# Two products of a graph layer by Strassen's scheme: seven products of quarters for eight, in stage 0 of a float32 kernel

## The chip, the cores and the metric

The kernel runs on one core of one Trainium2 chip. The metric is the device time of one execution in microseconds (us); less is better. The core has five queues that run side by side, each in its own order: PE (matrix products; PEld is its weight load), DVE (vector operations), ACT (activations), POOL (general operations, and one of the issuers of transfers) and SP (issues transfers). Matrix products land in PSUM[...]; everything else works in SBUF.

## The reference

Two graph attention layers over 4096 nodes with 512 features. Each normalizes its rows, takes the positive part, applies its attention and adds the result to its input. Only the first layer is touched, and of it the part before the attention:

```python
h = jnp.maximum(_layernorm(x, axis=-1), 0.0)       # rows, 4096 x 512
node_att = jax.nn.softmax(h @ node_w, axis=0)      # one weight a node
he = h @ edge_w                                    # 512 x 512 weights
e = jnp.where(adj > 0, he @ he.T, NEG_BIG)
edge_att = jax.nn.softmax(e, axis=1)
support = h @ weight                               # 512 x 512 weights
output = adj * (node_att * edge_att) @ support + bias
x = x + output
```

(The names h and he are changed here so that they agree with the kernel's.) The change concerns the two products `h @ edge_w` and `h @ weight`.

## The kernel before

The program has stages, one after the other: stage 0 (rows, the two products, node logits), stage B (scores of all pairs of blocks, from L289), stage C (softmax and attention of the first layer, from L364), and then the second layer. Each stage opens its own buffers in memory that the stage before has released.

Stage 0 is written with a fixed order: each queue executes what the Python code emits, in that order. The 4096 rows are 32 tiles of 128 rows (index t); four tiles make a block of 512 rows (index b, eight blocks). A tile goes through these functions:

- `fetch` (L130): SP loads the tile `xt` from `x`. There are 8 buffers.
- `stats` (L134): DVE computes mean and variance (L136, L138), ACT the deviation `sd` (L140).
- `norm` (L142): DVE computes `rs` and `mr` (L144, L146); ACT normalizes and takes the positive part in one activation, giving `h` (L149, L151).
- `logit` (L153): DVE multiplies `h` with the node weights and sums (`acc_z`, L154); POOL adds the bias to `xt` into a buffer `xb` (L157) and stores it (L158).
- Turning the tile so that features lie on the partitions. For the first two blocks (t < `T0` = 8) PE transposes and DVE copies (L188, L189). For the others `send` (L168) stores `h` in squares of 32, `pull` (L174) loads them back as `hq`, and DVE transposes inside the squares (L181). Both write into the block's tile `h_t`.

A finished block is then multiplied twice. `support(t)` (L192) makes one tile of `h @ weight`: four float32 matmuls of 512 columns into one bank, which DVE copies into `sup` (L198). `edges(b, d)` (L200) makes 128 features of `h @ edge_w`, turned, in the same way; ACT copies the bank into `he_t` (L205). Each product of a block has 16 matmuls of 512 columns. Banks come in three names (`pt`, `ps`, `pe`) with two buffers each.

`step(t)` (L216) places the tile work: around each `edges(b, j)` of block b it fetches, normalizes four tiles ahead, sends, turns one tile of block b+1, pulls two tiles ahead and takes statistics five tiles ahead. A block therefore is: four `edges` with four steps between, then the four `support` of the next block.

```python
for b in range(NB):
    for j in range(TB):
        edges(b, j)
        step((b + 1) * TB + j)
    if b + 1 < NB:
        for j in range(TB):
            support((b + 1) * TB + j)
```

Behind the loop come a few small operations on the node logits (L257 to L269), whose end releases the memory that the first loads of stage B use.

Of the functions that a comparison needs: L331 are the score matmuls of stage B; its tiles on the diagonal have 512, 384, 256 and 128 columns. L336, L343 and L344 are DVE's operations on these scores. L451 (DVE) and L461 (POOL) both use the result of the activation L445 in stage C.

Of the kernel before, what the change touches and what calls it, by code (L numbers as in the profile page):

```python
# [28 lines left out]
def kernel(  # L29
# [71 lines left out]
    with tc.tile_pool(name="w0", bufs=1) as wp, tc.tile_pool(name="a0", bufs=2) as ap_, tc.tile_pool(  # L101
        name="a0s", bufs=8
    ) as sp, tc.tile_pool(name="a0p", bufs=2, space=PSUM) as pp, tc.manual_schedule():
        we = wp.tile([P, KC, F], FP, name="we")
# [8 lines left out]

        pw = pp.tile([P, KC, P], FP, name="pt")
        for k in range(KC):
# [4 lines left out]
        T0 = 2 * TB  # L120
        nw_s = mb_0

        def squares_of(h):
# [6 lines left out]
        def fetch(t):  # L130
            xts[t] = sp.tile([P, F], FP, name="xt", bufs=8)
            nc.sync.dma_start(xts[t], x[t * P:(t + 1) * P, :])
# [9 lines left out]
        def norm(t):  # L142
            rs = sp.tile([P, 1], FP, name="rs")
            nc.vector.reciprocal(rs, sds.pop(t))  # L144
            mr = sp.tile([P, 1], FP, name="mr")
            nc.vector.scalar_tensor_tensor(mr, mvs.pop(t)[:, 0:1], -1.0, rs, op0=ALU.mult, op1=ALU.mult)  # L146
            hs[t] = sp.tile([P, F], FP, name="h", bufs=5)
            if t < T0:
                nc.scalar.activation(hs[t], xts[t], AF.Relu, bias=mr, scale=rs)  # L149
            else:  # L150
                nc.scalar.activation(squares_of(hs[t]), columns_of(xts[t]), AF.Relu, bias=mr, scale=rs)  # L151

        def logit(t, h):  # L153
            nc.vector.tensor_tensor_reduce(acc_z, h, nw_b if t < T0 else nw_s, 1.0, 0.0, ALU.mult, ALU.add,  # L154
                                           lg[:, t:t + 1])
            xb = sp.tile([P, F], FP, name="xb", bufs=1)
            nc.gpsimd.tensor_tensor(xb, xts.pop(t), bias_b, ALU.add)  # L157
            nc.gpsimd.dma_start(xb_d[t * P:(t + 1) * P, :], xb)  # L158
# [17 lines left out]
        def turn(t):  # L176
            b, j = divmod(t, TB)
            if j == 0:
                hts[b] = ap_.tile([P, KC, BL], FP, name="h_t")
            if t >= T0:  # L180
                nc.vector.transpose(  # L181
                    hts[b][:, :, j * P:(j + 1) * P].rearrange("p k (a q) -> p k a q", q=S),
                    hqs.pop(t).rearrange("p (a k q) -> p k a q", k=KC, q=S))
                return
            h = hs.pop(t)
            pt = pp.tile([P, KC, P], FP, name="pt")
# [13 lines left out]
        def edges(b, d):  # L200
            pe = pp.tile([P, BL], FP, name="pe")
            for k in range(KC):
                nc.tensor.matmul(pe, we[:, k, d * P:(d + 1) * P], hts[b][:, k, :],  # L203
                                 start=(k == 0), stop=(k == KC - 1))
            nc.scalar.copy(he_t[b][:, d, :], pe)  # L205


# [20 lines left out]
        upto(stats, 2)  # L228
        upto(norm, 1)
        turn(0)  # L230
        upto(stats, 3)
        upto(norm, 2)
        turn(1)
        support(0)
        upto(norm, 3)
        turn(2)
        support(1)
        upto(stats, 5)
        upto(norm, 4)
        turn(3)  # L240
        support(2)
# [17 lines left out]
        m2 = sp.tile([P, 1], FP, name="m2")  # L259
        nc.gpsimd.partition_all_reduce(m2, m1, P, bass_isa.ReduceOp.max)  # L260
        m3 = sp.tile([P, 1], FP, name="m3")
        nc.vector.tensor_scalar(m3, m2, -1.0, None, ALU.mult)
        s1 = sp.tile([P, 1], FP, name="s1")
        nc.scalar.activation(na, lg, AF.Exp, bias=m3, accum_out=s1)
        s2 = sp.tile([P, 1], FP, name="s2")
        nc.gpsimd.partition_all_reduce(s2, s1, P, bass_isa.ReduceOp.add)
        s3 = sp.tile([P, 1], FP, name="s3")
        nc.vector.reciprocal(s3, s2)
# [838 lines left out]
```

## Time and profile before

| what | value |
|---|---|
| device time, three runs | 2943.97, 2947.51 and 2948.33 us; median 2947.51 |
| the profiled execution | 2943.79 us; its span, first to last instruction, 2941.9 us |
| busy in the span | PE 2885.6, DVE 2536.9, ACT 1317.9, POOL 1410.4 us |
| stage 0, stretch 0 to 240.7 us | PE 227.84, PEld 103.15, DVE 102.13, ACT 52.37, POOL 61.53 us busy |
| L196 (`support`), L203 (`edges`) | 256 records each, 596 and 592 ns mean |

In the profile a line such as `L203 PE MATMUL pe<-h_t,we 128*128 128x512 f32 x256` is a group of instructions of one line of the kernel: its engine, what it writes and reads, its shape and count. A float32 matmul has two records. Records of PE overlap, since matmuls are pipelined, so the distance between starts tells more than the length of one. In a list in order of time the first number is the start in us from the span's start, the second the length; in brackets stands how long the engine was idle before and what it waited for. In a table of stretches each engine has its busy us and the number of its instructions; behind them stand the granted clock of PE (1.00 is full), the share of the transfer engines, and GB/s.

### The profile page before, as it was taken

What the parts mean: (1) busy time and instruction counts of PE and PEld (TensorE: products, weight loads), DVE (VectorE), ACT (ScalarE), POOL (GpSimd) and SP (SyncE); (2) the same over time, 40 slices, a digit from 0 to 9 for tenths busy, and PEclk for the clock granted to TensorE, in tenths of its full rate; (3) what the DMA queues carried; (4) which work ended last, traced back from release to release, by engine and by line L of the source; (5) the groups of instructions that cost most, each with busy time, mean ns of one, the idle gap of its engine ahead of it and who ended that gap; (6) DMA issues with size and microseconds to landing.
All of it is one profiled execution on the core that took longest, in us unless ns stands there. A gap on an engine that the chain in (4) does not pass through costs nothing.

```text
span 2941.9 us, 42890 instructions
## 1 busy us (share of the span) xinstructions
PE 2885.6 (98%) x14987; PEld 1144.6 (39%) x14987; DVE 2536.9 (86%) x3606; ACT 1317.9 (45%) x1817; POOL 1410.4 (48%) x1075
## 2 busy tenths in 40 slices
PE   8999999999999999999999989999999999999998
PEld 4444444444444444444444423333322223232223
DVE  5435777778898998998996789999999999999998
ACT  2211111111122222222221068888777777777776
POOL 3401111113444434444444756676766676767675
PEclk9999999999999999999999999999999999999999
DMA  5525666667877766756754269899989898999796
GB/s 182 172 79 201 223 218 224 226 218 182 208 169 194 189 158 199 193 159 189 203 168 136 58 181 237 239 225 239 232 236 233 238 233 236 234 237 235 209 227 168
DMA packets 517032, 587.66 MB, mean 200 GB/s; under 512 B 291832, under 2 KB 344088, under 8 KB 516816
## 3 DMA queue, kind: packets, MB, share of 16 engines
q1 hardware_dynamic: 460336, 410.90, 46.8%
q0 software_dynamic: 54464, 170.10, 26.1%
q10 hardware_dynamic: 2016, 3.93, 0.4%
q8 instruction: 117, 1.92, 0.3%
q14 instruction: 99, 0.81, 0.1%
HBM read 418.91 MB, written 73.60 MB: 167 GB/s over the span
## 4 chain that ended last, share of the span: by engine, by line
PE 73%; DVE 11%; ACT 7%; issue 4%; DMA 3%; POOL 1%; SPq 0%; DVEq 0%; ACTq 0%; POOLq 0%
PE po L481 28%; PE pe L331 15%; PE pv L886 14%; DVE pr L855 9%; PE dn L891 4%; PE po L592 4%; ACT e L823 3%; PE pe L203 3%; PE ps L196 3%; DMA acc<-pr 2%; ACT rl L841 1%; ACT ex L813 1%; DVE pr L852 1%; DMA xb_d<-xb 1%; DMA eb<-e_d 0%
## 5 line engine op out<-in xcount | busy, mean ns | idle before, releaser
L886 PE MATMUL pv<-pr,sup 128*32 128x512 f32 x8192 | 1023.6, 594 | 14.0 <-POOL d_m L1051 5.6
L481 PE MATMUL po<-sup,at 128*128 128x512 f32 x2048 | 884.1, 594 | 7.2 <-DMA eb<-e_d 6.1
L864 POOL TENSOR_TENSOR acc<-acc,pr 128x1024 f32<-128x1024 f32 x240 | 583.6, 2431 | 328.0 <-DVE pr L855 326.1
L855 DVE SCALAR_TENSOR_TENSOR pr<-z,g_m,ex 128x1024 f32<-128x1024 f32 x512 | 630.9, 1273 | 5.6 <-ACT ex L813 5.6
L481 PEld LDWEIGHTS po<-sup,at 128*128 128x128 f32 x2048 | 389.4, 191 | 493.8 <-issue 452.4
L461 POOL TENSOR_TENSOR racc<-racc,ex 128x512 f32<-128x512 f32 x240 | 354.2, 1476 | 388.2 <-ACT ex L445 386.8
L886 PEld LDWEIGHTS pv<-pr,sup 128*32 128x32 f32 x8192 | 300.8, 110 | 606.3 <-issue 509.3
L445 ACT ACTIVATE ex<-d 128x512 f32<-128x512 f32 x256 | 160.5, 630 | 611.5 <-DVE d L443 606.3
L331 PE MATMUL pe<-he_t,he_t 128*128 128x512 f32 x896 | 386.4, 592 | 0.0
L813 ACT ACTIVATE ex<-e 128x1024 f32<-128x1024 f32 x256 | 263.4, 1029 | 241.7 <-DVE pr L855 241.6
L891 PE MATMUL dn<-pr,d_m 128*2 128x512 f32 x1984 | 348.7, 592 | 0.0
L855 DVE SCALAR_TENSOR_TENSOR pr<-z,g_m,e 128x1024 f32<-128x1024 f32 x256 | 327.8, 1280 | 0.2 <-ACT e L823 0.2
L852 DVE SCALAR_TENSOR_TENSOR pr<-rl,ngd_m,ex 128x1024 f32<-128x1024 f32 x224 | 285.3, 1274 | 12.0 <-ACT ex L813 11.7
L823 ACT ACTIVATE e<-e,ld_m 128x1024 f32<-128x1024 f32 x256 | 291.3, 1138 | 0.0
L841 ACT ACTIVATE rl<-z,ngd_m,d_m 128x1024 f32<-128x1024 f32 x224 | 275.6, 1230 | 0.0
L335 POOL DMA_DIRECT2D e_d<-es x144 | 78.6, 546 | 364.6 <-ACT es L334 359.1
L331 PEld LDWEIGHTS pe<-he_t,he_t 128*128 128x128 f32 x896 | 169.6, 190 | 209.8 <-issue 190.4
L334 ACT COPY es<-pe 128x512 f32<-128x512 f32 (+2 forms) x144 | 79.1, 550 | 377.1 <-PE pe L331 377.1
L451 DVE TENSOR_TENSOR at<-ex,a 128x512 f32<-128x512 f32 x256 | 187.3, 732 | 66.9 <-ACT ex L445 41.6
L443 DVE TENSOR_TENSOR d<-pt,mk 128x512 f32<-128x512 f32 x256 | 177.0, 691 | 8.8
L336 DVE CUSTOM_DVE_ANT_0 mk<-pe,mk 128x512 f32<-128x512 f32 (+2 forms) x144 | 92.9, 645 | 98.8 <-ACT es L334 98.7
L870 POOL DMA_DIRECT2D acc<-pr x160 | 149.8, 936 | 2.5 <-DVE pr L855 1.5
(184 smaller groups left out, 2521.2 us busy)
## 6 DMA issues: line engine op xcount, KB each, us to landing
e<-in_adj_t_dram SPq DMA_DIRECT2D x256, 512.0 KB, 5.7
acc<-pr POOLq DMA_DIRECT2D x176, 512.0 KB, 5.6
a<-in_adj_t_dram SPq DMA_DIRECT2D x256, 256.0 KB, 4.0
ar<-in_adj_dram SPq DMA_DIRECT2D x120, 256.0 KB, 3.1
e_d<-es POOLq DMA_DIRECT2D x120, 256.0 KB, 3.1
eb<-e_d SPq DMA_DIRECT2D x456, 64.0 KB, 3.0
ac<-in_adj_t_dram SPq DMA_DIRECT2D x112, 256.0 KB, 3.7
et<-e_d SPq DMA_DIRECT2D x112, 256.0 KB, 5.1
```

Source lines behind the costliest of these rows:

```text
L331: nc.tensor.matmul(pe[:, :w], he_t[i][:, k, (t % TB) * P:(t % TB + 1) * P], he_t[j][:, k, BL - w:], start=(k == 0), stop=(k == KC - 1))
L451: nc.vector.tensor_tensor(w, e, aj.pop((b, m)), ALU.mult)
L461: nc.gpsimd.tensor_tensor(racc, racc, e, ALU.add)
L481: nc.tensor.matmul(po[j], w[:, j * P:(j + 1) * P], sup[:, m, :], start=(m == 0), stop=last)
L813: nc.scalar.activation(x_, ra.pop((i, m)), AF.Exp)
L823: nc.scalar.activation(x_, ra[i, m], AF.Exp, bias=ld_m[:, h // HG, m:m + 1])
L841: nc.scalar.activation(r, zs_[i, 0], AF.Relu, bias=ngd_m[:, h // HG, m:m + 1], scale=d_m[:, h, m:m + 1])
L852: nc.vector.scalar_tensor_tensor(w, rl.pop((i, m)), ngd_m[:, h // HG, m:m + 1], x_, op0=ALU.subtract, op1=ALU.mult)
L855: nc.vector.scalar_tensor_tensor(w, zs_[i, k], g_m[:, h + k, m:m + 1], e3.pop((i, m)) if k == 3 else x_, op0=ALU.max, op1=ALU.mult)
L864: nc.gpsimd.tensor_tensor(acc[i, 3], acc[i, 3], w, ALU.add)
L886: nc.tensor.matmul(v[c][q][r * D + c0:r * D + c0 + Q, :], va[:, m, g * HG + k, c0:c0 + Q], pr[i, m, k][:, q * BL:(q + 1) * BL], start=(m = ...
L891: nc.tensor.matmul(dn[r * Q:r * Q + w.shape[1], :], w, src[:, q * BL:(q + 1) * BL], **fl)
```

## The change

The first block stays as it was. From the second block on, each of the two products is cut into quarters: the block of rows into A11 to A22, the weights into B11 to B22, each 256 by 256. Seven products of quarters and sums of quarters, in the variant of Winograd, give the same result.

- `weight_sums` makes the sums of the weights' quarters, once, on POOL, in block 0; the last of them is written over a quarter of the weights when block 0 is done.
- `row_sums(b)` makes the four sums of the block's quarters on DVE. One overwrites the quarter A21; the others go into parts of `he_t` that are not filled yet, or for the last block into spare `xt` buffers.
- `product` is one product of quarters: four matmuls of 256 columns, into two halves of one bank.
- `parts_of` is the order of one product of a block: the first bank is copied by ACT to `u`, each other is added by DVE with what stands in SBUF, seven additions. After the 3rd, 6th, 9th and 11th of a block's 14 parts one `step` is emitted, and behind the last of these the row sums of the next block.
- All PSUM banks have one name, with eight buffers.
- To make room, there are 6 `xt` buffers (`XT`) for 8 and 4 of `h` for 5, and the bias is added to `xt` in place. `step` turns its tile first, and fetches after the send; the first fetches are spread over the opening.

```diff
         name="a0s", bufs=8
-    ) as sp, tc.tile_pool(name="a0p", bufs=2, space=PSUM) as pp, tc.manual_schedule():
+    ) as sp, tc.tile_pool(name="a0p", bufs=8, space=PSUM) as pp, tc.manual_schedule():
...
+        XT = 6
...
         def fetch(t):
-            xts[t] = sp.tile([P, F], FP, name="xt", bufs=8)
+            xts[t] = sp.tile([P, F], FP, name="xt", bufs=XT)
             nc.sync.dma_start(xts[t], x[t * P:(t + 1) * P, :])
...
-            hs[t] = sp.tile([P, F], FP, name="h", bufs=5)
+            hs[t] = sp.tile([P, F], FP, name="h", bufs=4)
...
         def logit(t, h):
             nc.vector.tensor_tensor_reduce(acc_z, h, nw_b if t < T0 else nw_s, 1.0, 0.0, ALU.mult, ALU.add,
                                            lg[:, t:t + 1])
-            xb = sp.tile([P, F], FP, name="xb", bufs=1)
-            nc.gpsimd.tensor_tensor(xb, xts.pop(t), bias_b, ALU.add)
+            xb = xts.pop(t)
+            nc.gpsimd.tensor_tensor(xb, xb, bias_b, ALU.add)
             nc.gpsimd.dma_start(xb_d[t * P:(t + 1) * P, :], xb)
...
         def support(t):
             b, j = divmod(t, TB)
-            ps = pp.tile([P, F], FP, name="ps")
+            ps = pp.tile([P, F], FP, name="bank")
             for k in range(KC):
...
+        LO, HI = slice(0, KC // 2), slice(KC // 2, KC)
+        L, R = slice(0, BL // 2), slice(BL // 2, BL)
+        Ts, As = {}, {}
+
+        def weight_sums(key, w, last=False):
+            B11, B12, B21, B22 = w[:, LO, L], w[:, LO, R], w[:, HI, L], w[:, HI, R]
+            if last:
+                nc.gpsimd.tensor_tensor(B12, B12, B11, ALU.subtract)
+                Ts[key].update({1: B11, 2: B21, 3: B22, 5: B12})
+                return
+            t2, t3 = (wp.tile([P, KC // 2, BL // 2], FP, name=f"{key}t{n}") for n in (2, 3))
+            nc.gpsimd.tensor_tensor(t3, B22, B12, ALU.subtract)
+            nc.gpsimd.tensor_tensor(t2, t3, B11, ALU.add)
+            Ts[key] = {6: t2, 7: t3}
+            if key == "s":
+                t4 = Ts[key][4] = wp.tile([P, KC // 2, BL // 2], FP, name="st4")
+                nc.gpsimd.tensor_tensor(t4, B21, t2, ALU.subtract)
+            else:
+                t4 = Ts[key][4] = [s.rearrange("p h t -> p (h t)") for s in (s_n, t_m)]
+                for k in range(KC // 2):
+                    nc.gpsimd.tensor_tensor(t4[k], B21[:, k, :], t2[:, k, :], ALU.subtract)
+
+        def row_sums(b):
+            ht = hts[b]
+            A11, A12, A21, A22 = ht[:, LO, L], ht[:, HI, L], ht[:, LO, R], ht[:, HI, R]
+            if b < NB - 1:
+
+                room = he_t[NB - 1 - b % 2]
+                s1, s2, s4 = room[:, LO, L], room[:, LO, R], room[:, HI, L]
+            else:
+                s1, s2, s4 = (spare() for _ in range(3))
+            nc.vector.tensor_tensor(s1, A21, A22, ALU.add)
+            nc.vector.tensor_tensor(s2, s1, A11, ALU.subtract)
+            nc.vector.tensor_tensor(A21, A11, A21, ALU.subtract)
+            nc.vector.tensor_tensor(s4, A12, s2, ALU.subtract)
+            As[b] = {1: A11, 2: A12, 3: s4, 4: A22, 5: s1, 6: s2, 7: A21}
+
+        def product(key, b, n):
+            acc = pp.tile([P, 2, BL // 2], FP, name="bank")
+            A, B = As[b][n], Ts[key][n]
+            for j in range(2):
+                js = slice(j * P, (j + 1) * P)
+                for k in range(KC // 2):
+                    Bk = B[k] if isinstance(B, list) else B[:, k, :]
+                    w, m = (A[:, k, js], Bk) if key == "s" else (Bk[:, js], A[:, k, :])
+                    nc.tensor.matmul(acc[:, j, :], w, m, start=(k == 0), stop=(k == KC // 2 - 1))
+            return acc
+
+        def result(key, b, r, c):
+
+            if key == "s":
+                return sup[:, b * TB + 2 * r:b * TB + 2 * r + 2, c * BL // 2:(c + 1) * BL // 2]
+            return he_t[b][:, 2 * c:2 * c + 2, r * BL // 2:(r + 1) * BL // 2]
+
+        def spare():
+            return sp.tile([P, F], FP, name="xt", bufs=XT).rearrange("p (k n) -> p k n", k=2)
+
+        def parts_of(key, b):
+
+            C = {(r, c): result(key, b, r, c) for r in range(2) for c in range(2)}
+            if key == "s":
+                u = nw_b.rearrange("p (k n) -> p k n", k=2)
+            else:
+                u = he_t[NB - 1 - b % 2][:, HI, R] if b < NB - 1 else spare()
+
+            def add(dst, x_, bank):
+                nc.vector.tensor_tensor(dst, bank, x_, ALU.add)
+
+            nc.scalar.copy(u, product(key, b, 1))
+            yield
+            add(C[0, 0], u, product(key, b, 2))
+            yield
+            add(u, u, product(key, b, 6))
+            yield
+            add(C[0, 1], u, product(key, b, 5))
+            yield
+            bank = product(key, b, 7)
+            add(C[1, 1], C[0, 1], bank)
+            add(C[1, 0], u, bank)
+            yield
+            add(C[0, 1], C[0, 1], product(key, b, 3))
+            yield
+            add(C[1, 0], C[1, 0], product(key, b, 4))
+            yield
...
         def step(t):
             if t < NT:
-                upto(fetch, t + 10 if t >= T0 else t + 7)
+                turn(t)
                 upto(norm, t + 4)
                 upto(send, t + 4)
-                turn(t)
+                upto(fetch, t + 9 if t >= T0 else t + XT)
                 upto(pull, t + 2)
                 upto(stats, t + 5)
...
-        upto(fetch, 7)
+        upto(fetch, XT - 1)
...
         turn(0)
+        upto(fetch, XT + 0)
...
-        upto(fetch, 9)
         upto(stats, 8)
         upto(norm, 7)
         nc.gpsimd.tensor_copy(squares_of(nw_s), columns_of(nw_b))
-        for b in range(NB):
-            for j in range(TB):
-                edges(b, j)
-                step((b + 1) * TB + j)
-            if b + 1 < NB:
-                for j in range(TB):
-                    support((b + 1) * TB + j)
-
-
-        m1 = sp.tile([P, 1], FP, name="m1")
+        weight_sums("s", ws)
+        weight_sums("e", we)
+        for j in range(TB):
+            edges(0, j)
+            step(TB + j)
+        weight_sums("s", ws, last=True)
+        weight_sums("e", we, last=True)
+        row_sums(1)
+        for b in range(1, NB):
+            n = 0
+            for key in "se":
+                for _ in parts_of(key, b):
+                    n += 1
+                    if n in (3, 6, 9, 11):
+                        step((b + 1) * TB + (3, 6, 9, 11).index(n))
+                    if n == 11 and b + 1 < NB:
+                        row_sums(b + 1)
+
...
```

More of the change, by code (lines that the diff above doesn't have):

```diff
@@ L112 @@
         nc.gpsimd.dma_start(bias_b, row_bcast(bias, F))
-        pw = pp.tile([P, KC, P], FP, name="pt")
+        pw = pp.tile([P, KC, P], FP, name="bank")
         for k in range(KC):
@@ L185, in turn @@
             h = hs.pop(t)
-            pt = pp.tile([P, KC, P], FP, name="pt")
+            pt = pp.tile([P, KC, P], FP, name="bank")
             for k in range(KC):
@@ L200, in edges @@
         def edges(b, d):
-            pe = pp.tile([P, BL], FP, name="pe")
+            pe = pp.tile([P, BL], FP, name="bank")
             for k in range(KC):
@@ L233 @@
         turn(1)
+        upto(fetch, XT + 1)
         support(0)
@@ L236 @@
         turn(2)
+        upto(fetch, XT + 2)
         support(1)
@@ L240 @@
         turn(3)
+        upto(fetch, XT + 3)
         support(2)
@@ L247 @@
         nc.gpsimd.tensor_copy(squares_of(nw_s), columns_of(nw_b))
[L248 to L257 removed]
+        weight_sums("s", ws)
[15 more added lines that the diff above has]
+                        row_sums(b + 1)
+        m1 = sp.tile([P, 1], FP, name="m1", bufs=1)
         nc.vector.tensor_reduce(m1, lg, AX.X, ALU.max)
[L259 removed]
+        m2 = sp.tile([P, 1], FP, name="m2", bufs=1)
         nc.gpsimd.partition_all_reduce(m2, m1, P, bass_isa.ReduceOp.max)
[L261 removed]
+        m3 = sp.tile([P, 1], FP, name="m3", bufs=1)
         nc.vector.tensor_scalar(m3, m2, -1.0, None, ALU.mult)
[L263 removed]
+        s1 = sp.tile([P, 1], FP, name="s1", bufs=1)
         nc.scalar.activation(na, lg, AF.Exp, bias=m3, accum_out=s1)
[L265 removed]
+        s2 = sp.tile([P, 1], FP, name="s2", bufs=1)
         nc.gpsimd.partition_all_reduce(s2, s1, P, bass_isa.ReduceOp.add)
[L267 removed]
+        s3 = sp.tile([P, 1], FP, name="s3", bufs=1)
         nc.vector.reciprocal(s3, s2)
```

## The prediction

> **What bounds the kernel now.** I read the chain of waits first, cut to the first 250 us, because the edit touches only stage 0. Columns: start us, length us, what.
>
> ```profile
> 53.57 0.59 DVE sup L198
> 54.16 0.04 issue
> 54.20 7.13 PE ps L196 x16
> 61.34 13.73 PE pe L203 x32
> ...
> 226.34 13.75 PE pe L203 x32
> 240.09 0.02 issue
> 240.11 0.59 ACT he_t L205
> ```
>
> Up to 53.6 us the chain hops between engines; from 54.2 to 240.1 us it is PE alone, blocks 1 to 7, 13.73 us for each product of a block, two products a block: 27.46 us. So 192 of the 240 us of the stage fall with PE's work, as long as nothing else takes over. Who could? The table of stretches, one product each (stretch, length, busy us of each engine):
>
> ```profile
> 116.47:130.20 13.73, 13.73 (x33) 6.09 (x33) 7.13 (x20) 4.46 (x8) 6.00 (x7) 1.00 0.55 173
> 130.20:143.94 13.74, 13.74 (x34) 6.10 (x33) 6.03 (x13) 1.87 (x4) 5.44 (x6) 1.00 0.58 191
> 198.87:212.60 13.73, 13.73 (x33) 6.09 (x33) 3.25 (x5) 1.75 (x3) 0.00 (x0) 1.00 0.12 38
> ```
>
> DVE is busy 13.2 us of a block's 27.5 in the middle of the stage (third figure), far less at its end, when the rows are used up. The change adds to DVE, so I need its real pace, waits included; the timeline of DVE shows one row tile:
>
> ```profile
> 72.89 0.16 DVE L144 RECIPROCAL rs<-sd 128x1 f32<-128x1 f32 x1 [0.36 <-ACT sd L140]
> 73.08 1.20 DVE L146 SCALAR_TENSOR_TENSOR mr<-mv,rs 128x1 f32<-128x1 f32 x1
> 75.21 0.69 DVE L154 CUSTOM_DVE_ANT_0 acc_z<-h,mb 128x512 f32<-128x512 f32 x1 [0.93 <-ACT h L151]
> 75.83 0.08 DVE L154 DVE_READ_ACCUMULATOR2_ANT lg<- 128x1 f32 x1
> 75.83 0.71 DVE L181 STREAM_TRANSPOSE h_t<-hq 128x512 f32<-128x512 f32 x1
> 76.46 0.65 DVE L136 BATCH_NORM_STATS2 st<-xt 128x6 f32<-128x512 f32 x1
> 77.14 0.18 DVE L138 BATCH_NORM_AGGREGATE mv<-st 128x2 f32<-128x6 f32 x1
> ```
>
> Start to start, a 512-wide operation costs 0.62 us although its record says 0.69. Between mr and acc_z DVE stands 0.93 us for ACT's 0.81 us activation; no later work fills that.
>
> **PE's part.** A block's product is now 7 x 4 matmuls of 256 columns instead of 16 of 512. Each float32 matmul is two records in the trace (L203: 256 records for 128 matmuls), and 32 records in 13.73 us are 0.429 us each. The 256-column case is already in this kernel: the diagonal tiles of L331.
>
> ```profile
> 695.57 2.78 PE L331 MATMUL pe<-he_t 128*128 128x256 f32 x16
> 698.19 0.27 PE L283 MATMUL pt<-ident,mx 128*4 128x128 f32 x1
> 704.58 4.98 PE L481 MATMUL po<-sup,at 128*128 128x512 f32 x6 [6.12 <-DMA eb<-e_d]
> ```
>
> The first row holds 8 records of 256 and 8 of 128 columns; next start minus start is 2.62 us. Scaling 0.429 by width gives 8 x (0.214 + 0.107) = 2.57, so an excess of 0.003 us a record: 0.216 us for 256 columns, each with its own weights. [...] By the row a quarter product is 8 x 0.216 = 1.726 us, seven are 12.08, a block 24.16 instead of 27.46. I take the row: same engine, type and weight load. If PE stays the bound it is 7 x 3.30 = 23.1 us less.
>
> **DVE's part, per block.** Removed: 4 copies of sup (DVE) and 4 of he_t (ACT). Added: 14 additions of a PSUM bank to SBUF, 2 ACT copies, 4 row sums.
> - Additions: L343, the same form, takes 0.685 us, 0.60 to 0.62 start to start, 0.72 if the next reads its result. 14 x 0.62 + 2 x 0.1 = 8.9 us.
> - Row sums: 4 x 0.62 + 0.1 = 2.6, plus 0.3 for the lock told below.
> - Four tiles: transpose 0.63, rs 0.19, mr to acc_z 1.09 with the wait for ACT, acc_z 0.62, statistics 0.79: 3.32 each, 13.3 us. The 0.36 us wait for sd goes, since the transpose now stands ahead of a norm whose sd is a step old.
> Sum 25.1 us; for semaphores of two-engine waits I add 0.2: **25.3 us against PE's 24.16**. DVE becomes the pace of blocks 1 to 5. Blocks 6 and 7 have no norms left: there PE paces.
>
> **The POOL lock.** [...] mr above took 1.20 us instead of 0.16 because xb ran from 73.00 to 74.26. Now xb is written in place, so it waits for the same ACT activation as acc_z. Stage C has that race:
>
> ```profile
> 1002.12 0.69 DVE L451 TENSOR_TENSOR at<-ex,a 128x512 f32<-128x512 f32 x1 [0.47 <-ACT ex L445]
> 1002.18 1.77 POOL L461 TENSOR_TENSOR racc<-racc,ex 128x512 f32<-128x512 f32 x1 [1.67 <-ACT ex L445]
> 1003.36 0.67 DVE L442 TENSOR_TENSOR pt<-pt,mb 128x512 f32<-128x512 f32 x1
> ```
>
> DVE is 0.06 us earlier and runs at its full 0.69; POOL pays (1.77, not 1.26). The bank addition L442 inside POOL's stretch is not delayed, so my 14 additions are not either. Only the first row sum, 1.4 us after acc_z, meets the end of POOL's 1.8: the 0.3 above.
>
> **Edits at nothing.** Copies u on ACT (0.57 us, ACT is 1/4 busy). Fewer xt buffers: fetch(t+9) waits on SP for the store of tile t+3, some 1.8 + 0.3 + 3.0 us after its activation, just under the 4.6 to 7 us to the next step; pull, behind it on SP, is used two steps later. h with 4 buffers: freed by the send of four steps ago. Eight PSUM banks under one name let PE run ahead; the cover gone would show as PE waiting for additions.
>
> **Block 0 to block 1, where the change costs.** Before, PE passes from block 0 to block 1 at 45.4 us and later loses 1.8 us on sup (L196 in the waits). Now block 1 needs row_sums(1), behind all of step(7) on DVE. DVE's steps 4 to 7 begin at 33.9 us (transposes after the first edges product). Each is copy 0.60, acc_z 0.60, rs and mr 1.28, acc_z 0.62, statistics 0.83: 3.9 us. POOL now works almost without a break (seven or so weight additions at 1.26 us from about 24 to 33 us, then eight xb with their stores at 2.1 us each), so in three of the four steps mr or acc_z waits about 0.8; and x tile 11, with six buffers, is fetched only when the store of tile 5 has landed (about 44 us) and comes 1.2 us late. 33.9 + 15.7 + 2.4 + 1.2 = 53.2; s1 and s2 of the row sums, 1.4 more: **54.6 us**. PE has its first two quarter products, which need no sums, done at 48.8 and stands 5.8 us. POOL's two last weight differences (54.4 to 57) come in time for the fourth product and cost a row sum 1.0 us.
> So long a stall meets the clock: after the 6.12 us wait at 704.58 above, the granted clock (third figure from the end) is 0.51 and about 2.2 us are lost:
>
> ```profile
> 704.50:709.00 4.50, 4.42 (x6) 1.88 (x7) 4.40 (x10) 0.63 (x1) 0.97 (x1) 0.51 0.64 99
> ```
>
> [...] by the chain it is nothing, because DVE paces blocks 2 to 5 and PE has caught up by block 4. I take nothing, and keep 2.2 for the range.
>
> **The sum.** Let s2(b) be the time at which block b's second row sum is there. s2(1) = 54.6. Row sums end at 57.0; up to s2(2) DVE has ten additions (6.4), four tiles (13.3) and two row sums (1.6): 78.3; PE reaches that point at 54.6 + 24.2 = 78.8. Then four DVE periods: s2(6) = 78.3 + 4 x 25.3 = 179.5. PE paces on: s2(7) = 179.5 + 24.2 = 203.7, and twelve products, 20.7, end at **224.4 us instead of 240.1: 15.7 us less**. The last addition takes the place of ACT's last copy (0.6 each); the softmax of the node logits then follows the last addition, and the first adjacency loads start 3.3 us after PE's end as now. Later stages only shift. The profiled execution took 2943.79 us (span 2941.9): 2928.1. The median of the runs is 3.7 above it, so I forecast 2931.8.
>
> **Rivals.**
> - PE keeps the pace (DVE period under 24.2): 54.6 + 6 x 24.16 + 20.7 = 220.3, 19.8 less, 2927.7. For it: DVE's start-to-start times may overlap more. Against: the sum above. 0.12.
> - DVE takes 27.5 us a block, from semaphore gaps or late hq and xt tiles behind a blocked SP queue: s2(6) = 188.3, end 233.2, 7 less, 2940.6. For it: six buffers, and 2.0 us for hq in the waits. 0.17.
> - Slower: POOL's xb takes the lock ahead of acc_z in each tile. Price: 1.1 us (acc_z took 1.53 instead of 0.69 at its worst, L451 up to 1.75). Four a block make 29.7 us; with four in block 0 and four in block 1, s2(2) = 87.1, s2(6) = 205.9, end 250.8: 10.7 slower, 2958. It decides from a DVE period of 29.2 us. Against it: L451 above. 0.10.
> [...]
> The forecast has 0.58; its own range, with the entry stall 4 us off either way, is 2926 to 2938.
>
> **Numbers.** About 0.2%, 5.9 us, is what a measurement of this kernel can tell from no change. Faster by more: the forecast, the first rival, half the second: 0.77. Within: the rest of the second and an odd forecast: 0.11. Slower: 0.12. Range 2925 to 2944: from just under the PE-paced case to the weak end of the second rival.
>
> **What would show it.** The quarter matmuls in stage 0 should be 0.216 us apart; PE idle about 5 to 6 us near 49 us, then about 1 us a block waiting for row sums, none in blocks 6 and 7; DVE busy over 80% from 57 to 180 us; acc_z near 0.69 and xb near 1.77; L331 first at about 225 us. Wrong if DVE shows long waits for DMA or POOL, if acc_z is near 1.7[...].

## The result and the profile after

| | before | after |
|---|---|---|
| device time, median of 6 | 2947.21 us (2943.97 to 2948.33) | 2934.49 us (2933.55 to 2939.02) |
| the profiled execution | 2943.79 us, span 2941.9 | 2933.75 us, span 2931.9 |
| PE ends stage 0 | 240.09 us | 230.87 us |
| PE starts stage B | 240.75 us | 231.73 us |
| PE busy in the whole span | 2885.6 us | 2866.7 us |

The ratio of the times is 0.9963 (95% interval 0.9953 to 0.9974): faster by 7.7 to 13.9 us, 10.9 in the middle. A second set of five runs gave 0.9964 (0.995 to 0.9977); in its trace the wait at the entry is 8.56 us and PE ends stage 0 at 230.77 us. The forecast was 15.7 us. In the two profiles the span is 10.0 us shorter, of which 9.0 lie before the start of stage B; the later stages differ by 1.0 us in total. So nothing is given back downstream, and the whole question lies in stage 0.

First the shape of it. PE's busy time fell by 18.9 us, but the span by 10.0 only: PE is idle 8.9 us more than before. The waits of PE in stage 0 of the kernel after say where (total, number, longest, us):

```profile
PE bank L265 <- DVE he_t L250: 11.1, 4, 8.6
```

L265 are the matmuls of `product`, L250 is the second row sum. One wait of 8.6 us, at the entry to block 1, and three of 0.85. The timeline of PE of the kernel after shows the long one and one of the short ones, and between them the distance of quarter products:

```profile
47.59 3.62 PE L265 MATMUL bank<-ws,h_t 128*128 128x256 f32 x16
59.78 3.48 PE L265 MATMUL bank<-st,he_t 128*128 128x256 f32 x8 [8.57 <-DVE he_t L250]
87.27 1.89 PE L265 MATMUL bank<-ws,he_t 128*128 128x256 f32 x8
89.00 1.89 PE L265 MATMUL bank<-st,h_t 128*128 128x256 f32 x8
90.73 1.89 PE L265 MATMUL bank<-ws,he_t 128*128 128x256 f32 x8
135.20 1.97 PE L265 MATMUL bank<-st,he_t 128*128 128x256 f32 x8 [0.85 <-DVE he_t L250]
```

From 87.27 to 89.00 to 90.73: 1.73 us a quarter product, eight records, 0.216 us each. The row of the forecast was right.

Next, the stretches of the kernel after. Each of the first three begins with a product that needs the row sums of its block, and is one block long (PE, PEld, DVE, ACT, POOL busy, granted clock, transfers):

```profile
85.55:109.94 24.39, 24.33 (x113) 21.12 (x112) 19.79 (x46) 5.37 (x10) 9.28 (x8) 1.00 0.58 172
135.20:160.46 25.26, 24.41 (x113) 21.20 (x113) 20.66 (x47) 5.37 (x10) 9.28 (x8) 1.00 0.55 167
185.72:209.97 24.25, 24.25 (x112) 21.36 (x113) 17.42 (x28) 1.17 (x2) 0.00 (x0) 1.00 0.15 42
59.60:62.00 2.40, 2.22 (x5) 1.83 (x6) 1.84 (x4) 0.00 (x0) 0.00 (x0) 0.50 0.09 36
```

In the middle of the stage a block takes 25.26 us, although PE needs 24.25 (third row, where there are no norms left): DVE paces, as forecast at 25.3. Note that DVE is "only" 82% busy (20.66 of 25.26) while it sets the pace. The last row is the short stretch behind the long wait: granted clock 0.50.

The chain of waits of the kernel after, at the end of the stage:

```profile
184.89 0.70 DVE he_t L250
185.59 0.14 issue
185.72 45.15 PE bank L265 x208
```

Before, PE alone carried the chain from 54.2 us on. Now it is PE for blocks 6 and 7 only; ahead of these rows, as far back as the view follows it (175.3 us), the chain alternates between DVE and ACT.

Where the entry went wrong is seen in the timelines of DVE and POOL of the kernel after, here DVE first:

```profile
55.64 0.66 DVE L249 TENSOR_TENSOR he_t<-h_t 128x512 f32<-128x512 f32 x1
56.33 3.30 DVE L250 TENSOR_TENSOR he_t<-he_t,h_t 128x512 f32<-128x512 f32 x1
```

```profile
56.59 1.27 POOL L224 TENSOR_TENSOR ws<-ws 128x512 f32<-128x512 f32 x1
57.81 1.27 POOL L224 TENSOR_TENSOR we<-we 128x512 f32<-128x512 f32 x1
```

The second row sum, an operation of 0.69 us, took 3.30: it ends when POOL's two last weight differences, which follow each other without a gap, are through (59.08), plus one operation of its own. By the records it starts 0.26 us ahead of the first of them and still stands; why it loses that start is not shown.

"Lock" is my name for what this trace shows in stage 0. DVE operations with two SBUF inputs that start while a POOL addition has at least 0.1 us to go take longer than the others of their kind: six of `mr` 0.23 to 1.19 us (0.16 otherwise), three of `acc_z` 0.85 to 1.75 (0.69), five of the first row sum 0.93 to 1.75 (0.66). Fifteen additions of a bank that start so take 0.66 us (0.65 to 0.69 otherwise), and 27 of the statistics 0.66 to 0.69.

### The profile page after: what moved, and what is told of

The parts are those of the page before. It is cut to its first block, busy times and chain, and to the rows that moved or that the text cites. A ratio compares the mean times of both kernels' runs of the same rounds, so it can differ in the third digit from the quotient of the medians.

```text
span 2931.9 us, 43759 instructions
## 1 busy us (share of the span) xinstructions
PE 2866.7 (98%) x15323; PEld 1220.3 (42%) x15323; DVE 2602.1 (89%) x3704; ACT 1311.0 (45%) x1803; POOL 1433.5 (49%) x1084
## 4 chain that ended last, share of the span: by engine, by line
PE 67%; DVE 11%; ACT 7%; issue 4%; DMA 2%; SPq 1%; POOL 1%; DVEq 0%; ACTq 0%; POOLq 0%
PE po L592 27%; PE pe L442 15%; PE pv L997 14%; DVE pr L966 9%; PE dn L1002 4%; PE po L703 4%; ACT e L934 3%; DMA acc<-pr 2%; PE bank L265 2%; ACT rl L952 1%; ACT ex L924 1%; DVE pr L963 1%; POOL acc L975 1%; SPq L520 1%; DVE pt L553 0%
## 5 line engine op out<-in xcount | busy, mean ns | idle before, releaser
L997 PEld LDWEIGHTS pv<-pr,sup 128*32 128x32 f32 x8192 | 308.6, 110 | 596.5 <-issue 494.7
```

Source lines behind the costliest of these rows:

```text
L997: nc.tensor.matmul(v[c][q][r * D + c0:r * D + c0 + Q, :], va[:, m, g * HG + k, c0:c0 + Q], pr[i, m, k][:, q * BL:(q + 1) * BL], start=(m = ...
```

## The experiments

All but the last two variants below ran once, beside the kernel before on the same chip (2947.37 us for 1, 2, 4 and the first form of 3; a median of 2945.7 for 5, 6, 7 and the second form of 3). Single times vary by a few us, so I read these runs by the moments in their traces, above all the moment at which PE ends stage 0 (after: 230.87; before: 240.09).

**1. Is it the order of DVE's work that makes its period 25.3?** In each tile DVE stands 0.93 us between `mr` and `acc_z` for ACT's activation. The norm is placed ahead of the transpose, so that the transpose fills that wait; the work is the same.

```diff
-                turn(t)
-                upto(norm, t + 4)
+                if t >= T0:
+                    upto(norm, t + 4)
+                    turn(t)
+                else: ...                  # order as it was
```

> From block 1 on, rs and mr of the row tile four ahead stand before the transpose, so that the transpose (0.63 us) runs inside the 0.93 us in which DVE stands for ACT. DVE's work is the same; 4 x 0.63 = 2.5 us of waiting leave a block. Theory 1 (DVE's order paces blocks 3 to 6, at 25.26 us between the first products that need row sums): its period falls to 22.8, below PE's 24.16, the three waits of 0.85 us go, the starts of those products are 24.2 us apart from block 2 on, and PE ends stage 0 at 227.5 us instead of 230.9. Theory 2 (PE paces, and the waits are only a remainder of the late entry and the half clock): spacing and end stay within 0.5 us.

Measured: 2929.7 us, PE ends at 227.14. The timeline of DVE in the kernel after, one tile, and then the same of this run:

```profile
89.44 0.70 DVE L183 STREAM_TRANSPOSE h_t<-hq 128x512 f32<-128x512 f32 x1
...
90.22 0.16 DVE L148 SCALAR_TENSOR_TENSOR mr<-mv,rs 128x1 f32<-128x1 f32 x1
91.31 0.69 DVE L156 CUSTOM_DVE_ANT_0 acc_z<-h,mb 128x512 f32<-128x512 f32 x1 [0.93 <-ACT h L153]
```

```profile
112.28 0.16 DVE L148 SCALAR_TENSOR_TENSOR mr<-mv,rs 128x1 f32<-128x1 f32 x1
112.36 0.70 DVE L183 STREAM_TRANSPOSE h_t<-hq 128x512 f32<-128x512 f32 x1
113.38 0.69 DVE L156 CUSTOM_DVE_ANT_0 acc_z<-h,mb 128x512 f32<-128x512 f32 x1 [0.31 <-ACT h L153]
```

The wait falls from 0.93 to 0.31, four times a block. The second row sums now follow each other in 24.17 us instead of 25.26, which is PE's own pace, and the three waits of 0.85 us on PE are gone. A stretch of a block of this run:

```profile
109.50:133.70 24.20, 24.20 (x114) 21.31 (x113) 20.81 (x47) 5.49 (x10) 9.28 (x8) 1.00 0.60 174
```

PE is busy through all of it. So DVE's serial waits for ACT made it the bound; 3.7 us of stage 0 hung on them (0.1 of it is an opening that happened to be earlier). How far DVE's own period fell, 22.8 by the expectation, cannot be read here, because PE now sets the distance.

**2. Is the long row sum due to POOL's two weight differences?** They are moved away from each other and from the row sums: that of `ws` directly behind the other weight sums, that of `we` into block 1.

```diff
         weight_sums("e", we)
+        weight_sums("s", ws, last=True)
...
-        weight_sums("s", ws, last=True)
-        weight_sums("e", we, last=True)
         row_sums(1)
...
+                    if (b, n) == (1, 3):
+                        weight_sums("e", we, last=True)
```

> POOL's two last weight differences are taken away from the entry to block 1: the one of the support weights is made early, behind the other weight sums, the one of the edge weights after the first step of block 1. Theory 1: the second row sum of block 1 stood behind these two back-to-back POOL operations (3.30 us instead of 0.69); it takes 0.7 us now, its end moves from 59.6 to 57.0 us, and since DVE's order carries this through, the stage ends 2.6 us earlier, at 228.3. Theory 2 (the row sum was long for another reason, a late tile or a wait on PE): it stays near 3 us.

Measured: 2929.78 us, PE ends at 228.75, 2.1 earlier than in the kernel after; 0.3 of it is an earlier opening (first quarter product at 47.29 instead of 47.59). DVE in this run:

```profile
56.39 0.69 DVE L250 TENSOR_TENSOR he_t<-he_t,h_t 128x512 f32<-128x512 f32 x1
```

0.69 instead of 3.30 us, and PE's wait at the entry is 6.32 instead of 8.57. The three short waits stay, so this is another part of the loss than that of the first experiment.

**3. What does the half clock behind the wait cost?** PE is kept busy through the wait by nine matmuls of 512 columns into a bank that nobody reads (extra work, no part of the computation).

```diff
             add(C[0, 0], u, product(key, b, 2))
+            if (key, b) == ("s", 1):
+                filler = pp.tile([P, F], FP, name="bank")
+                for k in range(9):
+                    nc.tensor.matmul(filler, hts[b][:, k % 2, 0:P], ws[:, k % KC, :],
+                                     start=(k == 0), stop=(k == 8))
```

> Nine matmuls of 512 columns, whose bank nobody reads, fill PE's wait of 8.6 us ahead of block 1's third product (7.7 us), so that the clock is not halved there. Their sum is no part of the output. Theory 1: block 1 on PE is 1.6 us shorter (24.2 instead of 25.8), but block 3 begins no earlier than DVE's row sums allow (109.8 instead of 109.94), and the stage ends within 0.4 us of 230.9. Theory 2 (the half clock is passed on to the end): the stage ends 1.6 us earlier, at 229.3.

Measured: 2939.33 us, PE ends at 236.9. This was a miss, by my own edit. The timeline of PE:

```profile
57.47 10.17 PE L294 MATMUL bank<-ws,h_t 128*128 128x512 f32 x18 [6.71 <-POOL ws L224]
```

The filler reads `ws`, which POOL's late difference still had to write. So it did not fill the wait: it sat it out and then ran in the path itself. It says nothing on the clock. Repeated with `he_t[0]` in place of `ws`:

> As the run before it, but the nine filler matmuls read the features of block 0 in place of the support weights, so that they don't wait for POOL's last weight difference and run inside PE's wait of 8.6 us (7.7 us of it). Their sum is no part of the output. Theory 1: full clock in block 1, the third products of blocks 1 and 2 are 24.2 to 24.9 us apart instead of 25.8, but from block 3 on DVE's row sums set the time as before: the stage ends within 0.4 us of 230.9, taken against the same end of the second row sum of block 1. Theory 2 (the half clock is passed on): 1.6 us earlier.

Measured: 2931.3 us, PE ends at 229.82. The timeline of PE:

```profile
51.09 7.89 PE L294 MATMUL bank<-he_t,h_t 128*128 128x512 f32 x18
59.85 1.96 PE L265 MATMUL bank<-st,he_t 128*128 128x256 f32 x8 [0.86 <-DVE he_t L250]
84.09 1.89 PE L265 MATMUL bank<-st,he_t 128*128 128x256 f32 x8
```

Now the row sums come at the same moment as in the kernel after (59.70 against 59.63), and PE shows no half clock: it covers the block in 24.24 us (59.85 to 84.09) instead of 25.77 (59.78 to 85.55). So the half clock cost PE 1.5 us. The end of the stage moves by 1.05. The result lies between the two expectations. Why the cost was not nothing although DVE paces is seen in the timeline of DVE, first in the kernel after, then in this run:

```profile
63.30 0.69 DVE L286 TENSOR_TENSOR nw_b<-bank,nw_b 128x512 f32<-128x512 f32 x1 [1.86 <-PE bank L265]
```

```profile
61.85 0.69 DVE L286 TENSOR_TENSOR nw_b<-bank,nw_b 128x512 f32<-128x512 f32 x1 [0.34 <-PE bank L265]
```

For the first additions after the row sums DVE itself waits for the slow products, 1.86 us against 0.34. The second row sum of block 2 ends at 84.53 in the kernel after and at 83.42 here: what DVE loses at the entry it does not make up.

**4. Is the gain due to fewer products at all?** All the other edits stay (one name for the banks, six `xt` buffers, the bias in place, the order in `step`, the first fetches), but the block loop is that of before, with plain `support` and `edges`, and without the sums of weights and rows.

```diff
-        weight_sums("s", ws)
...                                        # sums and parts
+        for b in range(NB):
+            for j in range(TB):
+                edges(b, j)
+                step((b + 1) * TB + j)
+            if b + 1 < NB:
+                for j in range(TB):
+                    support((b + 1) * TB + j)
```

> Only the two products go back to eight of quarters, that is to four matmuls of 512 columns a tile as before, without weight and row sums; eight banks under one name, six x buffers, the bias added in place, the new order in a step and the spread fetches stay. Theory 1: these side edits cost what the opening lost, some 2 us (PE reached block 1 at 47.6 instead of 45.4), partly given back because the 1.8 us wait for sup goes with eight banks: PE ends stage 0 at 240 to 241 us, before 240.1. Rival: the side edits themselves carry part of the gain or cost over 4 us: end below 238 or above 244.

Measured: 2945.24 us, PE ends at 239.67. The timeline of PE, the first and the last product of blocks 1 to 7, and then the first in the kernel before:

```profile
47.24 13.90 PE L198 MATMUL bank<-ws,h_t 128*128 128x512 f32 x32
...
225.77 13.90 PE L205 MATMUL bank<-h_t,we 128*128 128x512 f32 x32
```

```profile
45.37 7.03 PE L196 MATMUL ps<-ws,h_t 128*128 128x512 f32 x16
```

The side edits are worth 0.4 us at the end of stage 0, which is less than the opening varies between executions (last section). From block 1 on they save 2.3 us, most of it the 1.8 us wait for `sup`, and they lose 1.9 at the opening: block 1 begins at 47.24, where it began at 45.37 before. Of the 2.2 us by which the kernel after is late there (47.59), 1.9 thus come without any of the weight or row sums in it.

**5. What if the row sums do not wait for the norm and the statistics of the same step?** They are emitted directly behind the last transpose of a block.

```diff
                 turn(t)
+                if t % TB == TB - 1:
+                    row_sums(t // TB)
                 upto(norm, t + 4)
...
-        row_sums(1)
...
-                    if n == 11 and b + 1 < NB:
-                        row_sums(b + 1)
```

> The row sums of the next block are emitted straight behind its last transpose, ahead of the norm, logit and statistics of the tile four ahead (2.7 us on DVE with its wait for ACT). Work and buffers are the same. Theory 1: the second row sum of block 1 ends near 53.5 us instead of 59.6 (it may meet one POOL addition, 1.2 us), PE waits some 2.5 us instead of 8.6 and keeps its clock; DVE's period stays 25.3, so spacing from block 3 on stays 25.3, and the stage ends 4.5 to 5.5 us earlier, near 226. Theory 2 (PE paces from block 1 on): spacing 24.2 throughout and the full 6 us and more, end below 224.

Measured: 2929.72 us, PE ends at 227.45. The timeline of PE at the entry:

```profile
54.29 2.43 PE L265 MATMUL bank<-st,he_t 128*128 128x256 f32 x8 [3.20 <-DVE he_t L250]
60.52 3.78 PE L265 MATMUL bank<-ws,he_t 128*128 128x256 f32 x8 [3.79 <-POOL ws L224]
```

The wait for the row sums shrinks from 8.57 to 3.20 us, and a new one appears that it had covered: the fourth product needs POOL's difference of `ws`, which now stands behind a store and an addition of the bias on POOL. The entry is therefore no better: the third product of block 2 starts at 85.70, in the kernel after at 85.55. What moves the end by 3.4 us is the middle of the stage: DVE's period is still 25.15 us, but with the row sums 2.7 us earlier in each step PE starts each block with that much in hand and no longer waits for DVE, up to the end of the norms. This is another remedy for the same loss as that of the first experiment, not a further one.

**6. Is DVE the pace, or is it something that only goes with it?** DVE does the first of the two statistics operations of each tile twice from tile 13 on (extra work).

```diff
             nc.vector.bn_stats(st, xts[t])
+            if t > T0 + TB:
+                nc.vector.bn_stats(sp.tile([P, 6], FP, name="st", bufs=8), xts[t])
```

> Each tile from the fourteenth on has its statistics operation twice (0.62 us more on DVE a tile, 2.5 us a block, for blocks 1 to 5; the copy is not used). Theory 1: the period of DVE grows from 25.3 to 27.8 us and with it the spacing of blocks 3 to 6; the stage ends about 11.5 us later, at 242.4, which makes the kernel slower than before by 1 to 2 us. Theory 2 (PE paces): under 1.5 us later.

Measured: 2942.51 us, PE ends at 240.97. PE in this run:

```profile
113.91 1.97 PE L267 MATMUL bank<-st,he_t 128*128 128x256 f32 x8 [2.41 <-DVE he_t L252]
```

The waits of 0.85 us become 2.2 to 2.4, there are four of them now, and the second row sums follow each other in 26.83 us instead of 25.26 (27.8 was expected). The copy costs less than its start-to-start price of 0.62, because the operation behind it depends on the first one and had to stand a moment anyway: the statistics of a tile take 1.28 us instead of 0.83, which is 0.45 each, 1.8 a block; the first row sum no longer stands beside a POOL addition and gives 0.25 back (in the kernel after it took 0.93 us at the median, 0.66 at the least). Stage 0 ends 10.1 us later than in the kernel after. Of this 0.9 came with a later entry; 7.6 are the longer blocks on DVE (the third product of block 6 starts at 194.20 instead of 185.72, 8.5 later in all); the last 1.6 are a half clock that followed the wait ahead of that product (from there to the end PE takes 46.8 us instead of 45.2). So some 1.5 us a block on DVE, with what they bring in their train, undo the whole gain. Nothing but DVE's list was changed: DVE is the pace.

**7. The remedies together.** The norm first, the row sums directly behind the last transpose, and the two differences apart (experiments 1, 5 and 2).

> Three edits together: from block 1 on the norm ahead of the transpose, the two last weight differences away from the entry to block 1, and the row sums straight behind the last transpose. Theory 1: entry near 53.3 us without a half clock, then PE paces every block at 24.16: 53.3 + 6 x 24.16 + 20.9 = 219.2 us at the end of stage 0, 11.7 us less than the changed kernel and 21 us less than before; ratio to before 0.992 to 0.9935. Theory 2: DVE is not what held it, and the end is above 225.

Measured, in five rounds: 2927.72 us (2923.45 to 2928.32), ratio to before 0.9934 (0.992 to 0.9947). PE ends at 224.91, not at 219.2, just under the 225 of the second theory. The timeline of PE:

```profile
56.17 3.75 PE L265 MATMUL bank<-st,he_t 128*128 128x256 f32 x8 [3.62 <-DVE he_t L250]
```

After this 3.62 us wait PE never stands again, so DVE no longer holds it, and all that is missing lies before, in or just behind the wait: the first quarter product starts 1.3 us later than in the kernel after (48.93), the first row sum takes 1.91 us behind POOL's addition of a bias, and the half clock holds from 54.9 to 61.7 us. From the entry to the end PE takes 168.7 us.

**8. The same with four filler matmuls in the wait** (3.4 us of extra work, no part of the computation), against the half clock.

> The three edits together, and four filler matmuls of 512 columns (3.4 us, on features of block 0, their bank is read by nobody and no part of the output) inside the 3.6 us that PE waits at the entry to block 1. With all three edits PE paces every block, and the half clock there (2.75 us lost in the run before) has nothing to hide behind. Theory 1 (a lost PE time is passed on in full where PE paces, and only by what DVE must wait for a bank where DVE paces): no half clock, stage 0 ends 2.5 to 3 us earlier than 224.9 for the same entry, so the end minus the start of the first product needing row sums is 165.9 us instead of 168.7. Rival (the loss is absorbed here as well): it stays at 168.7.

Measured, in five rounds: 2924.71 us (2923.81 to 2926.51), ratio to before 0.993 (0.9917 to 0.9942). The kernel after ran on the same chip in the same rounds with 2934.56 us. The chain of waits:

```profile
53.48 0.70 DVE he_t L250
54.19 0.14 issue
54.32 166.06 PE bank L265 x768
```

One piece of 166.06 us, all of blocks 1 to 7 from the third product on: PE paces everything and ends 10.5 us before the kernel after. DVE runs ahead of it; its second row sums of blocks 2 and 3 are 23.3 us apart, less than PE's 24.2:

```profile
76.76 1.64 DVE L250 TENSOR_TENSOR he_t<-he_t,h_t 128x512 f32<-128x512 f32 x1
100.07 1.65 DVE L250 TENSOR_TENSOR he_t<-he_t,h_t 128x512 f32<-128x512 f32 x1
```

Against the 168.7 us of experiment 7 the half clock cost 2.7 us there, all of it in the stage, because no one else paces. The median is 9.9 us below that of the kernel after and 20.8 below that of the kernel before. That it is faster than experiment 7 is shown by the traces alone (these 2.7 us); the ratios of the times overlap. Of the 4.5 us between the ends of experiments 7 and 8 the other 1.8 lie in the opening and vary between executions (last section); they are no effect of the filler.

## Why the prediction was right, and where its sum was off

**Quarter products: right.** 1.73 us measured, 1.726 forecast; a block of PE 24.2. A slip in the sum is harmless: 0.2145 plus the excess of 0.003 is 0.2175 us a record, not 0.216, which would make 0.2 us a block.

**DVE becomes the pace: right in kind and size.** 25.26 us a block measured, 25.3 forecast (0.2 of it an allowance for semaphores that I had read from no trace); PE waits 0.85 us for the row sums of blocks 4, 5 and 6 and no more behind them; I had block 6 free of it already. Experiments 1 and 6 show both directions: 0.6 us less of waiting a tile on DVE hands the pace to PE, some 1.5 us more a block moves the end by 7.6 us, and by another 1.6 through the clock.

**The race for the lock between `acc_z` and `xb`: right.** `acc_z` has 736 ns on average (739 before), `xb` 1635 (1287 before). POOL pays, as in the row of stage C. The rival that makes the kernel slower fell with this. (Its turning point, a DVE block of 29.2 us, leaves out what this rival adds in blocks 0 and 1; with that it lies at 27.9. Nothing hangs on it.)

**The rest of the program only shifts: right,** to 1.0 us.

**The entry to block 1: its loss too small by 6.0 us, and the gain too large with it.** Forecast 54.6 us for s2(1), measured 59.6, 5.0 late; the half clock behind it makes another 1.0. Three terms of the sum were mis-sized. Together with 0.5 us in small pieces behind them they are the difference between 224.4 and 230.87:

- "33.9 + 15.7 + 2.4 + 1.2 = 53.2": the row sums began at 55.64, 2.4 late. The four steps themselves took 19.5 us against 19.3 (tile 11 came in time and tile 12 was 0.2 late, where I had 1.2; the lock took 3.3 instead of 2.4). It is the start of them, 36.17 us instead of 33.9, that was wrong: I took it over from the trace of before. Experiment 4 shows a delay of 1.9 us with the side edits alone. Part of it can be read in the traces: POOL's first addition of a bias, now in place and so behind an activation, runs beside the second tile's `mr`, which takes 0.96 us instead of 0.16, as the timelines of POOL and DVE of the kernel after show:

```profile
12.30 1.26 POOL L159 TENSOR_TENSOR xt<-xt,bias_b 128x512 f32<-128x512 f32 x1 [9.59 <-ACT h L151]
```

```profile
12.61 0.96 DVE L148 SCALAR_TENSOR_TENSOR mr<-mv,rs 128x1 f32<-128x1 f32 x1
```

  The first `support` on PE starts at 15.39 us instead of 14.53, 0.9 later, and its eight records take 5.14 us instead of 4.34, 0.8 more. By the estimate in the last section the 0.8 are an effect of the clock at the start, which varies between executions. No run put the bias back to separate the two. A wait of 0.3 us for `h_t` ahead of the fourth `support` comes with the weight sums; experiment 4 does not have it.
- "they cost a row sum 1.0 us": 2.6 in s2 alone. I had put the price of one POOL operation, and put it behind s2, where PE no longer waits for it. I let the two differences lie behind one another without asking what a waiting DVE operation gets in the seam; here it got nothing. Experiment 2 takes the two apart and gets 2.1 us back at the end of the stage, 0.3 of it by an earlier opening.
- "I take nothing" for the half clock: 1.0 us. The reasoning, that DVE paces and PE catches up, holds for later blocks, but at the entry DVE is waiting for PE. The 2.2 us that I kept for the range were too much: 1.5 were lost on PE and 1.05 at the end of the stage (experiment 3, second form).

The forecast of the time was 2.7 us under the median after, and this is a smaller error than that in the gain of stage 0, 6.5 us. That is luck: the later stages took 1.0 us off, and the median of these executions lies 0.7 above the profiled one, where I had added 3.7. By the end of stage 0 alone (230.87) the second rival's 233.2 was nearer than my 224.4; its cause, a DVE block of 27.5 us, is not what the traces show.

## What to carry to other kernels

When an engine takes over the pace while being 80% busy, look for its stalls behind a dependent operation on another engine and put independent work into them, before removing work; here swapping two lines was worth 3.7 us of a stage whose arithmetic saving was 23. A stage that is entered through a chain of hand-overs loses there what it gains in its steady part: cost the entry on the changed order of all queues, POOL's included, and do not carry the moments of the old trace over it. Two back-to-back POOL operations went with 3.30 us instead of 0.69 for a DVE operation with two SBUF inputs here; put such pairs where no one on the path needs DVE.

## What the runs showed of the hardware

**Half the clock behind a window in which PE was partly busy.** In the trace of the kernel after the granted clock changes at 56.03, 62.86, 694.32 and 701.15 us, after a first entry at 18.48: 11, 2, 185 and 2 times 3.413 us apart. At the entry to block 1 the window of 3.41 us ahead of the change to 0.50 has no PE work at all (52.62 to 56.03 us); the one before it is 59% busy (2.00 us), and the clock stayed at 1.00 behind it. The window ahead of a halving was not always empty. Here are stretches of experiment 5, and then of experiment 6, cut by such a grid (all but the second row):

```profile
52.24:55.65 3.41, 1.36 (x6) 1.25 (x7) 3.31 (x6) 0.00 (x0) 1.18 (x2) 1.00 0.91 303
60.50:65.80 5.30, 5.28 (x13) 4.16 (x14) 3.36 (x8) 1.11 (x2) 3.52 (x3) 0.50 0.58 172
```

```profile
112.19:115.60 3.41, 1.69 (x8) 1.54 (x9) 3.38 (x8) 0.77 (x2) 0.66 (x2) 1.00 0.79 192
190.69:194.10 3.41, 1.29 (x6) 0.79 (x5) 3.10 (x5) 0.72 (x2) 2.31 (x2) 1.00 0.36 91
194.10:197.51 3.41, 3.31 (x8) 2.71 (x9) 3.41 (x6) 0.00 (x0) 0.00 (x0) 0.50 0.46 147
```

In the first row of experiment 5 and the second of experiment 6 PE is busy for 1.36 and 1.29 of 3.41 us (40 and 38%), and the clock is half behind them. In experiment 5 PE had been running again for 1.36 us when the clock changed. The first row of experiment 6 is the window in which most of a wait of 2.41 us of that run falls, 23 steps of 3.41 us earlier: 1.69 us busy (50%), and the granted clock stayed at 1.00 behind it. So in this run a wait of 2.2 us (up to 194.20) went with the half clock and one of 2.41 us did not; they lie differently on the grid. The busy share of the window alone does not tell the two cases apart: at the end of the kernel before, a window with 1.82 us busy (53%, in matmuls of 8 and 128 columns) was followed by the half clock too. What decides is not shown. The half clock lasted 3.4 us in experiment 6; in the kernel after it lasted 6.83 us at the entry to block 1 and 13.65 in a later stage (1704.67 to 1718.32 us).

**Who gets the seam between two POOL additions.** The second row sum of block 1 stood through both differences of POOL, 3.30 us in the kernel after, and 3.33 to 3.35 in the five other traces with this order. But elsewhere in the same kernel a DVE operation with two SBUF inputs did get its turn between two POOL operations; POOL and DVE of the kernel after:

```profile
27.97 1.27 POOL L233 TENSOR_TENSOR st<-ws,st 128x512 f32<-128x512 f32 x1
29.20 1.72 POOL L228 TENSOR_TENSOR et<-we 128x512 f32<-128x512 f32 x1
```

```profile
28.44 1.35 DVE L156 CUSTOM_DVE_ANT_0 acc_z<-h,nw_b 128x512 f32<-128x512 f32 x1
```

`acc_z` waits for the first and runs ahead of the second, which takes 1.72 us instead of 1.27. In experiments 7 and 8 the same pair takes 1.36 and 1.72 us. What makes the difference is not shown. The most that such an operation took longer beside a single POOL addition in stage 0 is 1.25 us, in experiments 7 and 8 (the first row sum of block 1, 1.91 us instead of 0.66).

**The opening varies.** The first quarter product of block 1 started at 48.93 us in experiment 7 and at 47.09 in experiment 8, with the same code up to there. PE's timelines differ from the first `support` on, experiment 7 first and then 8:

```profile
15.78 6.08 PE L198 MATMUL bank<-ws,h_t 128*128 128x512 f32 x8
```

```profile
15.35 4.68 PE L198 MATMUL bank<-ws,h_t 128*128 128x512 f32 x8
20.30 3.60 PE L198 MATMUL bank<-ws,h_t 128*128 128x512 f32 x8
```

The same eight records take 6.08, 4.68 and, at full pace, 3.60 us. The column of the granted clock shows 1.00 in all of it, but only because the trace's list of granted clocks has no entry yet: it begins, with 1.00, at 20.77 us in experiment 7 and at 17.52 in experiment 8. For an estimate I take PE to run at half pace up to that entry. Then half of the time from the start of the records to the entry is lost: 3.60 + 2.50 = 6.10 and 3.60 + 1.09 = 4.69 us, against 6.08 and 4.68. It gives 5.15 for the kernel after (entry at 18.48, measured 5.14) and 4.34 for the kernel before (16.01, measured 4.34). By this estimate the slow opening is a half clock, which no trace records, and the moment at which it ends, the first entry, differs between executions: 17.5 to 20.8 us in the eleven traces with the side edits. Whether these edits have a share in its being later than in the one trace of the kernel before is open. A difference of 2 us between single runs of this kernel therefore tells nothing without the trace.
